# Batch 1's right-half product as seven half products, and a written-out order for all engines, in a gated cross-attention and FFN kernel

## The chip, the cores and the metric

The kernel runs on one core of one Trainium2 chip, in one launch. The metric is the device time of that launch in microseconds, the median of several runs. A profiled execution gives the trace; its span goes from the first to the last instruction of the program.

## What is computed

Two batches (`b` = 0, 1) of 1024 tokens with 2048 features go through two steps, both with a residual:

```python
x = x + tanh(g_xattn) * matmul(fake_quant(layernorm(x)), fake_quant(ctx))     # ctx: (2, 2048, 2048), one matrix for each batch
x = x + tanh(g_ffn) * scale * (x_ei @ kernel)                                  # x_ei: layernorm(x), its last 20% of features times -4
# fake_quant(v) = (clip(round(v / s + z), 0, 255) - z) * s
# kernel: (2048, 2048), of zeros and ones
```

"The first product" below is the one with the quantised context, "the second product" the one with the 0/1 matrix.

## The kernel before

The 16 tiles of 128 tokens are numbered `t` = 0 to 15 (8 to 15 are batch 1). Two neighbouring tiles form a pair `p`, two pairs a quad `q`. The result's columns are cut into four blocks `c` of 512; a half `h` is two blocks.

**First product, batch 0, and batch 1's right half (h = 1).** `load_x` brings a tile's rows, `stats` / `variance` / `square_root` / `factor` work out the layer norm (on VectorE, called DVE, and ScalarE, called ACT), `quant1` writes the quantised bytes, `turn1` transposes them on TensorE (PE), `take1` copies them from PSUM into an f16 tile `q1T`. `load_kv` and `quant_kv` do the same for the context; `fill_kv` on GpSimd (POOL) first clears the f16 tile that the bytes are written into. Column sums (`sums_mm` on PE, or `sums_pair` on DVE and `sums_last` on PE) and row sums (`rowsum1`, `rowsum1_pe`, then `tokb1`) correct for the zero points. `ops_unit` and `ops_several` give one unit of work: two tiles by one column block, 32 f16 matmuls of 128x512 (`mm1`), then for each tile `out1` (PSUM to SBUF, on ACT or DVE), `add_row1` and `add_out1` on POOL, `stats` for the second layer norm, and a store (`keep1`).

**First product, batch 1's left half (h = 0).** `ops_quad1` computes it with Strassen's scheme in Winograd's form: a pair of tiles and the two halves of the inner dimension make a 2x2 matrix of blocks, two column blocks and the same two halves another, and seven products of blocks (`mm1s`, M1 to M7) stand in for eight. `left_sum` and `right_sum` (DVE) make the sums and differences of blocks that these need. The seven products of a pair go into three PSUM sums X, Y, Z; after each product the running sum is added to where the scheme says: by `out1s` (ACT) and `add_out1` (POOL) for M2, M5, M4, M3, and by `take1s` (DVE) for M1, M6, M7.

**Second product.** `scale2`, `turn2` and `take2` normalise and transpose a tile (`A`); `combine` makes the left sums; `part_hi` (ACT) and `part_lo` (DVE or POOL) split each left block into two fp32r parts; `widen` (ACT) turns the bytes of the 0/1 matrix, or of its sums (`combine_w`), into fp32r; `mm2` runs seven products here too, in two passes (hi and lo). `add2` (DVE) adds a sum to rows loaded by `load_back`; `store2` writes them out.

**Memory.** SBUF holds 44 pages of 4 KB a partition, which all big tiles share. PSUM holds three accumulators of two banks each and two single banks for transposes and column sums.

**What sets the order.** The kernel first makes a list of steps: `op(...)` notes a step's engines with a cost on each, what it reads and writes, the pages it opens, and a due time. A planner in the kernel (`Plan.order`, `Plan.run`) then plays these steps through with those costs, 80 times with random changes of the due times, and keeps the order with the earliest end. Where a step may run on one of two engines, the planner chooses. The instructions are issued in that order, and each engine runs its own share strictly in turn; semaphores hold back what depends on another engine. All DMAs of the main part are issued from one queue, SyncE's (SP).

The lines that the prediction refers to by number:

```python
        nc.vector.tensor_sub(flat(out), flat(in0), flat(in1))                       # L609, right_sum
        nc.vector.scalar_tensor_tensor(xc, acc1[SUM[m], h, p // 2][:, p % 2, :], f1u, xc, ALU.mult, ALU.add)   # L658, take1s
```

L514 is `take1`, L544 `mm1`, L556 and L574 the column sums on PE, L646 `mm1s`, L692 `turn2`, L782 `widen`, L809 `mm2`, L825 `add2`.

Of the kernel before, what the change touches and what calls it, by code (L numbers as in the profile page):

```python
# [20 lines left out]
P = 128  # L21
# [8 lines left out]
class Op:  # L30
    __slots__ = ("engines", "f", "args", "deps", "users", "due", "lead", "opens", "uses",
                 "place", "end", "left", "index", "engine", "bias", "port", "ready")


class Plan:

    def __init__(self, buffers):
        self.free = dict(buffers)
        self.ops = []
        self.place = 0.0
        self.writer = {}  # L50
        self.readers = {}
        self.opener = {}
        self.kind = {}
        self.count = {}
        self.first = None

    def op(self, engines, f, *args, reads=(), writes=(), opens=(), main=False, due=None, lead=80, bias=0.0,
           port=False, in_turn=False):

        o = Op()
        o.engines, o.f, o.args, o.lead, o.index = engines, f, args, lead, len(self.ops)
        o.deps, o.users, o.uses, o.opens = set(), [], set(), []
        o.place, o.ready = None, 0.0
        o.due, o.bias, o.port = due, bias, port
        for kind, buf in opens:
            assert buf not in self.opener, buf
            self.opener[buf], self.kind[buf], self.count[buf] = o, kind, 0
            o.opens.append(buf)  # L70
        for key in reads:
            if key in self.writer:
                o.deps.add(self.writer[key])
            self.readers.setdefault(key, []).append(o)
            o.uses.add(key[0])
        for key in writes:
            if key in self.writer:
                o.deps.add(self.writer[key])
            o.deps.update(self.readers.pop(key, ()))
            self.writer[key] = o  # L80
            o.uses.add(key[0])
        for buf in o.uses:
            if buf in self.opener:
                o.deps.add(self.opener[buf])
                self.count[buf] += 1
        if in_turn:
            if self.first is not None:
                o.deps.add(self.first)
            self.first = o
        o.deps.discard(o)  # L90
        for d in o.deps:
            d.users.append(o)
        if main:
            o.place = self.place
            self.place += min(engines.values())
            o.due = o.place if due is None else due
        self.ops.append(o)
        return o

    def dues(self):  # L100
        inf = float("inf")
        given = [o.due for o in self.ops]
        for o in reversed(self.ops):
            d = inf if o.due is None else o.due
            for u in o.users:
                if u.place is not None or u.due is not None and u.due < inf:
                    d = min(d, (u.due if u.place is None else u.place) - min(o.engines.values()) - 3)
            o.due = d
        for o, g in zip(self.ops, given):
            if o.due == inf:  # L110
                o.due = max([d.due for d in o.deps] + [0.0]) + 50

    def order(self, lag, start, runs, seed=1):


        self.dues()
        chance = random.Random(seed)
        free, count = dict(self.free), dict(self.count)
        dues = [o.due for o in self.ops]
        best = None  # L120
        for i in range(runs):
            self.free, self.count = dict(free), dict(count)
            try:
                end = self.run(lag, start)
            except RuntimeError:
                end = None
            if end is not None and (best is None or end <= best[0]):
                best = end, self.began, [o.engine for _, _, o in self.began]
                dues = [o.due for o in self.ops]
                held = self.held_up()  # L130
            for o, due in zip(self.ops, dues):
                o.due = due
            for ops in held:
                if chance.random() < 0.5:
                    step = chance.choice((3.0, 6.0, 12.0, 24.0))
                    for o in ops:
                        o.due -= step
            if i % 3:
                place = chance.uniform(0.0, self.place)
                for o in self.ops:  # L140
                    if o.place is None and abs(o.due - place) < 120.0 and chance.random() < 0.1:
                        o.due += chance.uniform(-25.0, 25.0)
        _, self.began, engines = best
        for (_, _, o), e in zip(self.began, engines):
            o.engine = e
        return [o for _, _, o in self.began]

    def held_up(self):

        before, begin, all_ = {}, {}, []  # L150
        for s, _, o in self.began:
            begin[o] = s
            last = before.get(o.engine)
            before[o.engine], before[o] = o, last
            if o.place is None or last is None or s - begin[last] - last.engines["PE"] < 1.0:
                continue
            ops = []
            x = o
            for _ in range(8):
                x = self.rel.get(x)  # L160
                if x is None or x.place is not None:
                    break
                ops.append(x)
                p = before.get(x)
                if p is not None and begin[p] + p.engines[p.engine] > x.ready + 1.0:
                    break
            all_.append(ops)
        return all_

    def run(self, lag, start):  # L170


        self.rel = {}
        ready = {}
        events = []
        began = []
        for o in self.ops:
            o.left = len(o.deps)
            o.end = 0.0
        tick = 0  # L180

        def push(time, what, o):
            nonlocal tick
            tick += 1
            heappush(events, (time, tick, what, o))

        for o in self.ops:
            if not o.left:
                for e in o.engines:
                    push(0.0, "ready", (e, o))  # L190
        done = set()
        engines = sorted({e for o in self.ops for e in o.engines}, key=lambda e: (e != "PE", e))
        for e in engines:
            ready[e] = []
        busy = {e: e in start for e in engines}
        for e, time in start.items():
            push(time, "idle", e)
# [82 lines left out]
def gated_xattn_ffn_kernel(  # L280
# [885 lines left out]
    for q in (2, 3):  # L1166
        ops_quad1(0, q)
# [62 lines left out]
```

## Time and profile before

| | |
|---|---|
| median of 3 runs | 698.88 us (698.78 to 699.11) |
| span of the profiled execution | 697.0 us |
| PE busy | 674.0 us, 97% |
| PE weight loads | 471.7 us, beside the matmuls |
| DVE busy | 490.2 us, 70% |
| ACT busy | 455.4 us, 65% |
| POOL busy | 316.8 us, 45% |
| moved by DMA | 155.78 MB, 223 GB/s over the span |

The page gives the profiled execution by its span; the runs' median lies 1.9 us above that. The time of any one run lies within 0.3 us of the median. A span's stages by the start of their first instruction: the first matmul at 13.2 us; the second product of batch 0 from 145 us on; batch 1's first product from 367 us on (its right half mostly between 408 and 476 us); its second product from 476 us on. In groups of instructions, the time after the bar is what the group was busy, then the mean of one instruction in ns, then the idle time of the engine before it and what ended that. Instructions that follow each other on DVE and ACT overlap a little, so busy time over count is what one costs its engine, and the mean is what one lasts. In windows the columns are the length, then busy time (and count) of PE, its weight loads, DVE, ACT and POOL, the granted clock, the DMA share and GB/s.

### The profile page before, as it was taken

Reading aid. Unit: us, or ns where it says so; the run is one execution under the profiler, and the core shown is the slowest. Engines: PE = TensorE matmul, PEld = TensorE weight load, DVE = VectorE, ACT = ScalarE, POOL = GpSimd, SP = SyncE. Lnnn points to the kernel's source line nnn. Section 1 sums busy time; section 2 is a strip of 40 time slices with the busy share of each in tenths; the row PEclk is TensorE's granted clock in tenths of the full one; section 3 lists DMA queues with packets and bytes.
Section 4 is the critical chain, followed back from the end, with each engine's and each line's share of the span. In section 5 each row is a group of like instructions: output and inputs, shape, how many; then the busy total and the mean of one; then the engine's idle time right before and its main releaser. Section 6 shows DMA issues by size and latency. Waiting matters only on the chain.

```text
span 697.0 us, 8833 instructions
## 1 busy us (share of the span) xinstructions
PE 674.0 (97%) x3180; PEld 471.7 (68%) x3180; DVE 490.2 (70%) x717; ACT 455.4 (65%) x536; POOL 316.8 (45%) x210
## 2 busy tenths in 40 slices
PE   1999999989999999999999999999999999999997
PEld 0444444468788888878885444447888888888885
DVE  6899958899998886497878888468572425583331
ACT  4599444286888566699926768229699347689540
POOL 8166789863625221855717887975120101040000
PEclk9999999999999999999999999999999999999999
DMA  8999406777995799477379677327074379155032
GB/s 302 393 393 380 162 13 231 259 261 251 361 400 225 233 324 339 140 247 278 120 263 330 222 268 245 121 92 275 27 260 162 105 231 324 67 170 222 22 131 90
DMA packets 63580, 155.78 MB, mean 223 GB/s; under 512 B 4912, under 2 KB 21296, under 8 KB 63536
## 3 DMA queue, kind: packets, MB, share of 16 engines
q1 hardware_dynamic: 63536, 155.21, 62.9%
q8 instruction: 25, 0.41, 0.2%
q14 instruction: 19, 0.16, 0.1%
HBM read 117.44 MB, written 37.75 MB: 223 GB/s over the span
## 4 chain that ended last, share of the span: by engine, by line
PE 87%; DMA 4%; DVE 4%; POOL 2%; ACT 2%; issue 1%; SPq 0%; ACTq 0%; DVEq 0%
PE acc_M L809 57%; PE acc L544 19%; PE acc_M L646 7%; PE tr L692 4%; DMA kv<-in_kv_dram 3%; DMA x<-in_x_dram 1%; POOL x L596 1%; DVE wB L767 1%; ACT wf_M L782 1%; POOL x L592 1%; PE tr L503 1%; DVE qn L472 0%; PE cs L574 0%; DVE x L685 0%; DVE bn_b L426 0%
## 5 line engine op out<-in xcount | busy, mean ns | idle before, releaser
L809 PE MATMUL acc_M<-wf_M,hi_M 128*128 128x512 f32 x896 | 282.0, 395 | 1.6 <-ACT wf_M L782 1.5
L809 PE MATMUL acc_M<-wf_M,lo_M 128*128 128x512 f32 x896 | 277.6, 390 | 0.6 <-POOL lo_M L742 0.6
L782 ACT ACTIVATE wf_M<-wr_M 128x1024 fp32r<-128x1024 uint8 x224 | 221.6, 1050 | 26.8 <-DMA wr_M<-in_wmask_dram 24.2
L809 PEld LDWEIGHTS acc_M<-wf_M,lo_M 128*128 128x128 f32 x896 | 168.0, 188 | 36.8 <-POOL lo_M L742 1.3
L809 PEld LDWEIGHTS acc_M<-wf_M,hi_M 128*128 128x128 f32 x896 | 164.1, 188 | 34.4 <-ACT wf_M L782 3.2
L544 PE MATMUL acc<-q,q1T 128*128 128x512 f16 x768 | 171.6, 381 | 1.2 <-DVE q1T L514 0.8
L825 DVE SCALAR_TENSOR_TENSOR back<-acc_M,f,back 128x1024 f32<-128x1024 f32 (+1 forms) x58 | 72.1, 1245 | 124.7 <-PE acc_M L809 117.1
L742 POOL TENSOR_TENSOR lo_M<-A,hi_M 128x1024 fp32r<-128x1024 f32 x24 | 62.1, 2586 | 179.5 <-ACT hi_M L738 160.1
L544 PEld LDWEIGHTS <-q1T 128*128 128x128 f16 x768 | 75.2, 98 | 90.2 <-issue 1.9
L592 POOL TENSOR_TENSOR x<-x,row 128x512 f32<-128x512 f32 x64 | 88.6, 1408 | 43.8 <-ACT sd_a L438 15.5
L596 POOL TENSOR_TENSOR x<-x,e 128x512 f32<-128x512 f32 x64 | 92.0, 1458 | 30.6 <-ACT e L586 16.1
L738 ACT CAST hi_M<-A 128x1024 fp32r<-128x1024 f32 x48 | 50.1, 1044 | 13.1 <-POOL A L726 4.7
L530 ACT ACTIVATE q<-kv,sc,rs 128x1024 uint8<-128x1024 f32 x45 | 53.5, 1236 | 7.8 <-DMA kv<-in_kv_dram 5.1
L586 ACT ACTIVATE e<-acc,tokb,f1u 128x512 f32<-128x512 f32 x34 | 25.1, 774 | 49.6 <-PE acc L544 47.8
L426 DVE BATCH_NORM_STATS2 bn_b<-x 128x6 f32<-128x512 f32 x64 | 43.1, 684 | 15.9 <-POOL x L596 15.6
L495 ACT COPY A<-tr 128x512 f32<-128x512 f32 x35 | 20.3, 584 | 46.5 <-PE tr L692 45.8
L742 DVE TENSOR_TENSOR lo_M<-A,hi_M 128x1024 fp32r<-128x1024 f32 x24 | 33.7, 1421 | 7.2 <-ACT hi_M L738 7.2
L568 DVE TENSOR_TENSOR pair<-pair,q 128x1024 f16<-128x1024 f16 x36 | 36.6, 1022 | 2.5 <-ACT q L530 0.8
L728 POOL TENSOR_TENSOR A<-A,A 128x1024 f32<-128x1024 f32 x8 | 21.1, 2648 | 23.7 <-DVE A L726 16.4
L522 POOL MEMSET q<- 128x1024 f32 x32 | 29.2, 952 | 5.1 <-DVE q L532 2.2
L512 ACT ACTIVATE q1T<-tr 128x1024 f16<-128x1024 uint8 x22 | 21.3, 1019 | 7.5 <-PE tr L503 6.8
L767 DVE SCALAR_TENSOR_TENSOR wB<-wB,wB 128x2048 uint16<-128x2048 uint16 x8 | 24.2, 3031 | 0.0
(103 smaller groups left out, 594.1 us busy)
## 6 DMA issues: line engine op xcount, KB each, us to landing
kv<-in_kv_dram SPq DMA_DIRECT2D x64, 512.0 KB, 9.2
x<-in_x_dram SPq DMA_DIRECT2D x32, 512.0 KB, 7.7
x<-x SPq DMA_DIRECT2D x32, 512.0 KB, 3.0
back<-x SPq DMA_DIRECT2D x32, 512.0 KB, 6.1
wr_M<-wt_T SPq DMA_DIRECT2D x32, 512.0 KB, 5.6
out_dram<-back SPq DMA_DIRECT2D x30, 512.0 KB, 3.6
wr_M<-in_wmask_dram SPq DMA_DIRECT2D x24, 512.0 KB, 5.4
n<-in_x_dram SPq DMA_DIRECT2D x16, 512.0 KB, 7.2
```

The costliest lines, as they stand in the source:

```text
L426: nc.vector.bn_stats(bn[v, t][:, c, :], xt[src[v, t, c // 2]][:, ts(c % 2, NB)])
L530: nc.scalar.activation(low, v, AF.Identity, bias=z2, scale=rs2)
L544: nc.tensor.matmul(acc1[b, c, tiles[0]][:, i, :], q1T[tiles[i]][:, k, :], rhs1(b, c, k), start=(k == 0), stop=(k == KT - 1),)
L568: nc.vector.tensor_add(colsum[b, c], colsum[b, c], v[:, i : i + 2, :])
L592: nc.gpsimd.tensor_add(xc, xc, colrow[b, c])
L596: nc.gpsimd.tensor_add(xc, xc, ev.pop((t, c)))
L646: nc.tensor.matmul(acc1[key][:, i, :], left_half(p, LEFT1[m])[:, 4 * s + k, :], right1(m, h, s)[:, k, :], start=(m in OPENS and s == 0 and ...
L738: nc.scalar.copy(hi[m, p], A[left(m, p)])
L742: engines[engine].tensor_sub(lo[m, p], A[left(m, p)], hi[m, p].bitcast(F32))
L782: nc.scalar.activation(wf[q, m, k], wr[q, m, k // 4][:, k % 4, :], AF.Copy, bias=-float(RIGHT[m][1]))
L809: nc.tensor.matmul(acc2[SUM[m], p][j], part[m, p][:, k, :], wf[q, m, k][:, ts(j, NB)], start=(m in OPENS and k == 0 and part is hi), stop= ...
L825: nc.vector.scalar_tensor_tensor(v, acc, f2, v, ALU.mult, ALU.add)
```

## The change

Two things are changed together.

1. `ops_quad1` is called for both halves of batch 1, and `ops_right_sums(1, ...)` makes the right sums of the right half; the units (`ops_unit`) of that half and the early loads of its x tiles go. A tile's left sums, made once for the left half, are used again.
2. The planner is taken out of the kernel. `Plan` still notes the steps with their dependencies, but issues them in the order of a table, `ORDER_OF_OPS`, of 2326 step numbers; a letter behind a number says which engine takes a step that may run on two (D, A, P). Costs, due times and the limits on pages are no longer looked at.

The list of steps is otherwise the same: 2314 before, 2326 after (64 `mm1` and 16 `out1` go; 56 `mm1s`, 16 `out1s`, 12 `take1s` and 8 `right_sum` come). The order of the steps in the table is not that of the planner before.

```diff
-    def __init__(self, buffers):
-        self.free = dict(buffers)
+    def __init__(self):
...
-    def dues(self):
...
-    def order(self, lag, start, runs, seed=1):
...
-    def held_up(self):
...
-    def run(self, lag, start):
...
+    def run(self, order):
+
+        names = {"D": "DVE", "A": "ACT", "P": "POOL"}
         done = set()
...
+        for word in order.split():
+            o = self.ops[int(word.rstrip("DAP"))]
+            assert o not in done and o.deps <= done
+            done.add(o)
+            if len(o.engines) > 1:
+                o.f(*o.args, engine=names[word[-1]])
             else:
...
+                o.f(*o.args)
+        assert len(done) == len(self.ops)
+
+
+ORDER_OF_OPS = """
+0 1 33 16 17 90 32 40 149 35 37 38 48 195 42 3 43 2 45 207 4 5 143 47 18 85 6 19 7 87 95 8 213 59 34A 155 20 9A
+84 229 41D 137 21 10A 58 22 23 36A 11 24 89 12A 231 50 44D 25A 220 13D 221 92 39A 26D 14 52 49A 46D 222 223 15
...
-    plan = Plan(dict(page=PAGES, acc=3, tr=2, qn=QN, row=4, e=3, pair=2))
+    plan = Plan()
...
     for c in range(2, NC):
         ops_kv(1, c, 200.0, False)
+    ops_right_sums(1, 200.0)
     pairs = ops_batch(1, "x", True)
-    for q in (2, 3):
-        ops_quad1(0, q)
-    for t in range(TPB, T):
-        v = ("x", t, 1)
-        op({"SP": DMA}, load_x, v, t, 1, writes=both(v), opens=[("page", v)], lead=60)
-    for some in (pairs[:2], pairs[2:]):
-        for c in range(2, NC):
-            for tiles in some:
-                ops_unit(1, c, tiles)
+    for h in range(2):
+        for q in (2, 3):
+            ops_quad1(h, q)
     ops_left(2, (False, False))
     ops_product2(2, {4: [(ops_left, (3, (True, True)))]})
     ops_product2(3, {})
 
-    order = plan.order({("ACT", "SP"): 8.0, ("POOL", "SP"): 12.0, ("DVE", "SP"): 12.0, "PE": 6.0, "ACT": 1.5, "DVE": 1.5, "POOL": 1.5, "SP": 4.0, "DMA": 10.0,
-                        ("PE", "PE"): 0.0}, {"SP": 13.0, "DVE": 22.0, "ACT": 22.0}, 80, 2)
-    for o in order:
-        if len(o.engines) > 1:
-            o.f(*o.args, engine=o.engine)
-        else:
-            o.f(*o.args)
+    plan.run(ORDER_OF_OPS)
```

## The prediction

> **What bounds it now.** I read the page's shares first, then the chain that ended last in order of time, then the windows, then the forms of VectorE (DVE), and last the built order of both kernels.
>
> ```profile
> PE 674.0 (97%) x3180; PEld 471.7 (68%) x3180; DVE 490.2 (70%) x717; ACT 455.4 (65%) x536; POOL 316.8 (45%) x210
> ```
>
> TensorE (PE) is busy for 97%. Its steady paces are in the chain and the timeline:
>
> ```profile
> 42.74 1.13 DVE q1T L514
> ...
> 77.99 18.99 PE acc L544 x88
> ...
> 506.40 70.77 PE acc_M L809 x312
> ```
> ```profile
> 13.23 1.01 PE L556 MATMUL cs<-q,ones_h 128*128 128x512 f16 x2 [13.23 <-ACT q L530]
> ...
> 19.06 2.61 PE L544 MATMUL acc<-q,q1T 128*128 128x512 f16 x6
> ...
> 692.60 0.75 DVE L825 SCALAR_TENSOR_TENSOR back<-acc_M,f,back 128x512 f32<-128x512 f32 x1 [1.06 <-PE acc_M L809]
> ```
>
> One f16 matmul takes 18.99 / 88 = 0.2158 us, one of the second product 70.77 / 312 = 0.2268; eight transposes take 0.87 in the chain, 0.109 each; 16 row sums 0.54, 0.034 each. PE's whole list at these paces: 1792 x 0.2268 + (768 + 224 + 44) x 0.2158 + 320 x 0.109 + 32 x 0.034 = 406.4 + 223.6 + 34.9 + 1.1 = 666.0. The last eviction starts at 692.6, so PE ends 26.6 us "late" against its list. I follow that lateness by counting the matmuls ahead of a place: 13.2 before the first matmul; 20.0 at 44.6 us (the first matmuls take 2.61 / 6 = 0.43, and PE waits for the DVE step in the chain at 42.74); still 20.1 at 138.3 (tile 0's first transposes); 23.7 at 254.6 (tile 6's first transposes); 26.6 at the end. After the first 45 us PE loses 6.6 us in all. Nothing else can give much: the end is 697.0 - 692.6 = 4.4 of eviction and store.
>
> Second thing to see: how well DVE can be filled.
>
> ```profile
> 25.00:75.00 50.00, 48.45 (x258) 22.96 (x257) 48.07 (x95) 42.91 (x46) 29.09 (x22) 1.00 1.02 381
> 75.00:125.00 50.00, 50.00 (x237) 23.21 (x236) 37.81 (x94) 20.03 (x31) 41.47 (x34) 1.00 0.36 125
> 150.00:200.00 50.00, 48.47 (x236) 39.42 (x235) 48.71 (x67) 40.48 (x51) 22.81 (x10) 1.00 0.94 329
> ```
>
> Third column of time is DVE. Pressed (first and third row) it is busy 96.78 of 100 us, idle 3.3% of its busy time; unpressed (second) it idles 32%. In the first 25 us it is busy 18.38, of which 1.8 are constants: it starts 8.4 us behind its list.
>
> **What goes and comes on PE.** The right half took 4 pairs x 2 columns x 32 = 256 matmuls (64 steps of 4); as seven products it takes 4 x 7 x 8 = 224 (56 steps). 32 x 0.2158 = 6.9 us leave PE, and PE sets the end. The rest of its list is the same. This is the whole gain of the arithmetic; 1.0% of 698.88.
>
> **What the seven products add.** The left half shows all of it.
>
> ```profile
> L658 DVE SCALAR_TENSOR_TENSOR x<-acc_M,f1u,x 128x512 f32<-128x512 f32 x12 | 8.5, 744 | 4.5 <-PE acc_M L646 2.2 <-issue 2.2
> ...
> L609 DVE TENSOR_TENSOR q2T<-q,q 128x2048 f16<-128x2048 f16 x2 | 6.8, 3430 | 0.0
> ...
> L609 DVE TENSOR_TENSOR q<-q,q 128x2048 f16<-128x2048 f16 x2 | 2.4, 1218 | 0.0
> ```
>
> DVE gets 12 take1s (8.5) and 8 right sums, at 1.22 each alone or 3.43 beside a 2.6 us GpSimd (POOL) subtraction: 9.8 to 27.4. I take 1.75, the mean of the eight here: 14.0. The 16 out1 of the right half (12 on ACT, 4 on DVE) become 16 out1s on ACT (11.7 us); POOL's adds stay 32. Pages: six more for the sums, 44 in all as before. Place: between the second column sum of batch 1 (C: PE list 324.5) and its second product (445.4) PE has 120.9 us, and in the new order DVE has 105 to do there with the right sums at 1.75. With the eight at 3.43 it is 119: still under PE, so I cost the additions at nothing; PE is the cover. Without the cover (DVE already behind at C) they would cost up to their 22.5. PSUM: 28 evictions instead of 16, each product of a sum waiting for the one before; the left half's two quads raise PE's lateness by 0.5 us (25.1 to 25.6), so 0 to 0.5 here, taken as 0.
>
> The Trainium skill, "SBUF — State Buffer", section "Who interferes with whom", speaks against these sums: a DVE instruction with two SBUF inputs and a GpSimd instruction that reads SBUF exclude each other for a whole instruction. The stage is POOL's busiest, but its adds there last 1.4 us, so by the rule a sum costs up to an estimated 2.7, less than the 3.43 seen.
>
> **The order table.** No instruction keeps its place after the first few: the order is new on all engines, from the first microseconds. DVE goes from 490 to 527 steps, ACT from 513 to 495: beyond the 20 steps above, DVE takes over quantising of kv (19 to 26), of x (11 to 16), take1 (10 to 16) and take2 (16 to 25), and gives up 7 out1 (those four among them) and 2 row sums. With busy/count of the forms (stats 0.65, quant kv 1.05, quant x 1.33, take1 1.19, row sum 2.26, out1 0.81, pair sums 0.87 and 2.03, scale2 1.19, lo part 1.37, combine 1.54, weight sum 3.03, add2 1.28, factor 1.70 and 0.80, variance 0.41, tokb 0.24, take2 0.68) the old list sums to 510.9 where the engine was busy 490.2, as neighbours overlap: factor 0.96. The new list is 548.9 x 0.96 = 527: below PE's 659.1. Whole sums do not decide; what is due when does. So I add up what DVE must have done before a given PE step: in DVE's new queue, everything up to the last instruction that the step waits for, directly or through other engines:
>
> - A, tile 0's transposes, now after 400 f16 matmuls instead of 524: PE list 91.3. DVE: 50 stats 32.5, 10 variances 4.1, factors 14.4, 10 kv 10.5, 8 take1 9.5, 6 quant 8.0, 3 row sums 6.8, 6 out1 4.9, pair sums 13.9, 2 scale2 2.4, 6 tokb 1.4: 108.4 x 0.96 = 104.1.
> - B, tile 6's transposes: PE list 228.6. DVE: 93 stats 60.5, variances and factors 37.5, 10 kv 10.5, 12 quant 16.0, 9 take1 10.7, 5 row sums 11.3, pairs 13.9, 10 tokb 2.4, 7 out1 5.7, 15 scale2 17.9, 8 weight sums 24.2, 7 lo 9.6, 5 combines 7.7, 5 take2 3.4, 12 add2 15.4: 246.6 x 0.96 = 236.7 (before: 214.0 at list 230.9).
>
> DVE reaches a place at 8.4 + list x (1 + idle share). At 3.3%: A at 116.0, PE lateness at least 116.0 - 91.3 = 24.7; B at 253.0, lateness 24.4; C (322.7) at 341.8, 17.3. So the new order makes DVE, not PE, the pace of the first 115 us: 4.6 us more lateness at A than the 20.1 there now. What PE lost between A and B (3.6) I take as hidden by that, since ACT and POOL gain the same 4.6. What it lost after B is 2.9; the transposes that caused part of it are spread differently now, so between 0 and 2.9: I take the middle, 1.5. End: 24.7 + 1.5 = 26.2 against 26.6.
>
> Loads: the 47th DMA (kv of column 2) is needed at PE list 49.5, that is at 69.5 with lateness 20. The windows move 331, 393 and 369 GB/s per 25 us, so 47 x 0.524 MB are in at about 68, and quantised 1.24 later: just in time. One load later costs 0.5 / 0.37 = 1.4 us. A new wait on SP would hold all loads behind it; the DMA count is unchanged.
>
> **Sum**, against the profiled execution (span 697.0; the runs' median lies 1.9 above): 697.0 - 6.9 - 0.4 + 1.9 = 691.6. Own range: idle share 2.6% (third row), nothing lost after B: lateness 23.9, -2.7, so 689.3; idle share 4.0% (first row) and 2.9 lost: B 26.0, lateness 28.9, +2.3, so 694.3.
>
> **Rivals.**
> 1. DVE becomes the bound (slower). The price: at B each 1% of idle share is 2.4 us on PE. 6.9 + 26.6 - 1.5 = 32.0 of lateness at B eats the gain; that is an idle share of 6.5%. For it: 105 us of the old order idle at 32% or near, because in-order DVE waits for POOL and ACT, and two operand forms grow from 1.2 to 3.4 beside POOL. Against it: 3.3% in pressed windows. At 8%: B at 264.0, lateness 36.9, +3.4: 702.3. Between 4% and 6.5% the time is 694 to 699.
> 2. DVE is less pressed than my averages (its conversions fall where POOL idles: 0.8 instead of 1.2). Then PE's lateness stays near 20.1 and gets at most the 2.9: 685.5 to 689.
> 3. The change does not do what it says: the 28 evictions hold PE. At 0.5 us for each of 14 products it gives the 6.9 back: about 699. The left half says 0.5 for the same number.
>
> The Trainium skill, "TensorE: Matmul & The Clock Gate", part 1, adds a risk to rival 1: after about 3.4 us of idleness PE runs at half rate for as long again. By it a relapse would cost an estimated 3.4 us. Here only the start shows the half pace; waits of up to 1.4 us later (ACT wf_M) brought none back.
>
> **Numbers.** Forecast 0.62; rival 2 0.14; milder DVE waits (694 to 699) 0.11; rival 1 0.10; rival 3 0.03. About 0.2% can be told from no change (697.5 to 700.3). Faster 0.83, same 0.05, slower 0.12. Range 687.5 to 699.0.
>
> **Checks.** In the profile after: 512 f16 matmuls of the plain form and 448 of the sevens; DVE busy about 527 and over 95% up to 115 us; tile 0's transposes at about 116, tile 6's at about 253; PE from C to the second product without gaps. I am wrong if PE waits for DVE several us near B, or if kv loads end its waits at 45 to 75 us.

## The result, and the profile after

The changed kernel takes 715.57 us, the median of four runs (711.99 to 717.09), against 698.86 us before: 1.0232 times as long, with a 95% interval of 1.0206 to 1.0257. The forecast was 691.6, with a range of 687.5 to 699.0. The profiled execution took 711.99 us with a span of 709.9: it is the fastest of the four, so that 3.6 of the median's 16.7 us stand in no trace. One execution of the first kernel below took 1166 us and one of the kernel with norms later 1782, and as these were the traced ones, the times of these two kernels are medians of the other three and no lateness is given for them.

The page's busy times, after:

```profile
PE 670.9 (95%) x3148; PEld 467.1 (66%) x3148; DVE 506.3 (71%) x753; ACT 445.0 (63%) x521; POOL 324.5 (46%) x211
```

32 matmuls fewer on PE, as foreseen, and no other engine that is near full. The chain that ended last, as shares of the span by engine, before and then after:

```profile
PE 87%; DMA 4%; DVE 4%; POOL 2%; ACT 2%; issue 1%; SPq 0%; ACTq 0%; DVEq 0%
```
```profile
PE 60%; DVE 16%; DMA 15%; issue 3%; ACT 2%; POOL 2%; SPq 1%; DVEq 0%
```

Before, PE carried the chain almost alone. After, DVE and loads carry a third of it, with little more work to do. The chain in order of time shows how (start, length, what):

```profile
94.06 6.04 PE acc L447 x28
...
264.40 5.08 DMA n<-in_x_dram
269.69 8.46 DMA y<-x
278.18 0.81 DVE y L588
...
409.44 5.20 DMA kv<-in_kv_dram
414.71 1.10 issue
415.81 1.44 ACT e L568 x2
417.32 1.58 POOL x L499
418.90 0.90 POOL q L425
419.82 1.25 ACT q L433
422.00 8.49 DMA kv<-in_kv_dram
...
664.52 41.11 PE acc_M L712 x180
```

The paces are those of before: 6.04 / 28 = 0.2157 and 41.11 / 180 = 0.2284 us a matmul. Between them stand relays: a load, a step of DVE, the next load (264 to 279 us), or a load of kv, an eviction, an add of GpSimd (POOL), a zero fill, a quantization, another load (409 to 430 us). No relay holds PE for long, since there is always some other product to run, but each costs a little: PE's waits in the whole execution, apart from the 13.2 us of the start, are some thirty that the trace names, none over 2.0 us.

The three stretches that the prediction read for DVE's idle share, and the two ends of PE's work:

```profile
25.00:75.00 50.00, 45.95 (x231) 21.28 (x229) 46.10 (x86) 38.23 (x42) 29.24 (x21) 1.00 1.03 391
75.00:125.00 50.00, 48.54 (x233) 22.98 (x233) 48.31 (x93) 20.35 (x29) 39.99 (x30) 1.00 0.41 139
150.00:200.00 50.00, 47.76 (x226) 38.26 (x224) 40.85 (x70) 34.40 (x43) 25.98 (x13) 1.00 0.71 244
```
```profile
13.18 1.01 PE L459 MATMUL cs<-q,ones_h 128*128 128x512 f16 x2 [13.18 <-ACT q L433]
...
705.65 0.75 DVE L728 SCALAR_TENSOR_TENSOR back<-acc_M,f,back 128x512 f32<-128x512 f32 x1 [1.06 <-PE acc_M L712]
```

DVE's idle share is 8.5%, 3.5% and 22% of its busy time. The rows of the added work (after, both halves together):

```profile
L561 DVE SCALAR_TENSOR_TENSOR x<-acc_M,f1u,x 128x512 f32<-128x512 f32 x24 | 17.5, 741 | 3.1 <-POOL x L495 2.4 <-PE acc_M L549 0.6
L512 DVE TENSOR_TENSOR q2T<-q,q2T 128x2048 f16<-128x2048 f16 x8 | 11.6, 1455 | 1.6 <-PE acc_M L712 1.4 <-PE acc_M L549 0.2
L512 DVE TENSOR_TENSOR q2T<-q,q 128x2048 f16<-128x2048 f16 x4 | 6.8, 1695 | 0.0
L512 DVE TENSOR_TENSOR q<-q,q 128x2048 f16<-128x2048 f16 x4 | 6.5, 1656 | 0.0
```

The sums are cheap: (11.6 + 6.8 + 6.5) / 16 = 1.56 us each where 1.75 had been taken.

The prediction's own measure reads best: PE's lateness, that is the start of a PE step less the sum of PE's list ahead of it. The table below gives it at places of the list, worked out from the traces in the same way as there and good to some 0.2 us (units: the right half as it was; sevens: as in the change). The right half's products stand at 382 to 445 of the list (to 450 with units), with the left half's last ones among them, up to 396.

| kernel | 100 | 150 | 250 | 345 | 375 | 405 | 435 | 460 | 655 | time |
|---|---|---|---|---|---|---|---|---|---|---|
| before (units) | 20.1 | 22.9 | 24.2 | 25.1 | 25.6 | 25.6 | 25.6 | 25.6 | 26.3 | 698.9 |
| after (sevens) | 25.3 | 28.3 | 35.2 | 36.7 | 37.1 | 39.7 | 41.9 | 43.0 | 46.2 | 715.6 |

6.9 us of matmuls are saved and 46.2 - 26.3 = 19.9 us of lateness are added (13.0 together, which is what the profiled execution is longer), spread over the whole program: the two differ by 5.2 at 100, 11.0 at 250, still 11.5 at 375, then 16.3 at 435 and 19.9 at the end.

### The profile page after: what moved, and what is told of

Read it like the earlier page. It is cut to its first block, busy times and chain, and to the rows that moved or that the text cites. A ratio compares the mean times of both kernels' runs of the same rounds, so it can differ in the third digit from the quotient of the medians.

```text
span 709.9 us, 8788 instructions
## 1 busy us (share of the span) xinstructions
PE 670.9 (95%) x3148; PEld 467.1 (66%) x3148; DVE 506.3 (71%) x753; ACT 445.0 (63%) x521; POOL 324.5 (46%) x211
## 4 chain that ended last, share of the span: by engine, by line
PE 60%; DVE 16%; DMA 15%; issue 3%; ACT 2%; POOL 2%; SPq 1%; DVEq 0%
PE acc_M L712 44%; PE acc L447 7%; DMA kv<-in_kv_dram 7%; PE acc_M L549 6%; DMA y<-x 4%; PE tr L595 3%; DVE pair L471 3%; DMA x<-in_x_dram 3%; DMA n<-in_x_dram 2%; DVE bn_b L329 2%; ACT wf_M L685 1%; DVE back L728 1%; DVE q2T L512 1%; POOL x L499 1%; DVE bn_a L329 1%
## 5 line engine op out<-in xcount | busy, mean ns | idle before, releaser
L645 POOL TENSOR_TENSOR lo_M<-A,hi_M 128x1024 fp32r<-128x1024 f32 x23 | 56.4, 2454 | 208.6 <-ACT hi_M L641 142.5
L495 POOL TENSOR_TENSOR x<-x,row 128x512 f32<-128x512 f32 x64 | 94.7, 1495 | 53.9 <-ACT row L481 34.8
L447 PE MATMUL acc<-q,q1T 128*128 128x512 f16 x512 | 116.7, 381 | 1.8 <-ACT q L433 1.4
L499 POOL TENSOR_TENSOR x<-x,e 128x512 f32<-128x512 f32 x64 | 96.9, 1526 | 31.8 <-ACT e L489 13.7
L447 PEld LDWEIGHTS <-q1T 128*128 128x128 f16 x512 | 49.9, 98 | 61.0 <-issue 1.9
L433 ACT ACTIVATE q<-kv,sc,rs 128x1024 uint8<-128x1024 f32 x38 | 46.7, 1238 | 35.4 <-DMA kv<-in_kv_dram 33.1
L549 PEld LDWEIGHTS <-q1S 128*128 128x128 f16 x256 | 24.9, 98 | 30.8 <-DVE q1S L533 1.4
L329 DVE BATCH_NORM_STATS2 bn_b<-x 128x6 f32<-128x512 f32 x64 | 42.3, 680 | 0.0
L489 ACT ACTIVATE e<-acc,tokb,f1u 128x512 f32<-128x512 f32 x25 | 19.3, 772 | 25.3 <-PE acc L447 22.7
L549 PEld LDWEIGHTS <-q1T 128*128 128x128 f16 x192 | 18.7, 98 | 23.7 <-issue 2.4
L568 ACT ACTIVATE e<-acc_M,tokb,f1u 128x512 f32<-128x512 f32 x32 | 23.5, 769 | 15.0 <-POOL x L499 8.9
L435 DVE TENSOR_SCALAR q<-kv,rs,sc 128x1024 uint8<-128x1024 f32 x26 | 26.0, 1010 | 7.9 <-DMA kv<-in_kv_dram 7.1
```

What stands on the lines that cost most here:

```text
L329: nc.vector.bn_stats(bn[v, t][:, c, :], xt[src[v, t, c // 2]][:, ts(c % 2, NB)])
L433: nc.scalar.activation(low, v, AF.Identity, bias=z2, scale=rs2)
L447: nc.tensor.matmul(acc1[b, c, tiles[0]][:, i, :], q1T[tiles[i]][:, k, :], rhs1(b, c, k), start=(k == 0), stop=(k == KT - 1),)
L495: nc.gpsimd.tensor_add(xc, xc, colrow[b, c])
L499: nc.gpsimd.tensor_add(xc, xc, ev.pop((t, c)))
L549: nc.tensor.matmul(acc1[key][:, i, :], left_half(p, LEFT1[m])[:, 4 * s + k, :], right1(m, h, s)[:, k, :], start=(m in OPENS and s == 0 and ...
```

## Experiments

Two things were changed together, so the theories were: **1**, the sevens are a gain and the table's order is what costs; **2**, the sevens of the right half cost more beside PE than they save, whatever the order; **3**, the table gives DVE too much work. All of before's times in these runs lie at 698.7 to 698.9. Where an experiment changes the order alone, the table of steps is what changes, and a few words of it stand for the diff.

### Is it the table?

**Sevens, but ordered by the planner of before:**

```diff
     for c in range(2, NC):
         ops_kv(1, c, 200.0, False)
+    ops_right_sums(1, 200.0)
...
-    for q in (2, 3):
-        ops_quad1(0, q)
...
+    for h in range(2):
+        for q in (2, 3):
+            ops_quad1(h, q)
```

> Both halves as seven products, the order made by the planner of before (80 tries, its costs unchanged). Theory 1, the written-out order is what costs and the seven products are a gain: 698.9 less 6.9 of matmuls plus 0 to 3 of new waits, 692 to 695, and PE's lateness against its list stays near 27 us. Theory 2, the seven products of the right half cost more than they save (28 evictions, 8 right sums on VectorE): 703 or more, with PE's waits gathered in batch 1's first product.

712.97 us (1.0201, 1.0183 to 1.0220). Theory 1 missed by some 20 us: without the table the sevens are as slow.

**The table's order and engines with units in the right half** (64 unit steps where the 56 products stood, steps that they need pulled forward):

```diff
-    ops_right_sums(1, 200.0)
...
-    for h in range(2):
-        for q in (2, 3):
-            ops_quad1(h, q)
+    for q in (2, 3):
+        ops_quad1(0, q)
...
+    for some in (pairs[:2], pairs[2:]):
+        for c in range(2, NC):
+            for tiles in some:
+                ops_unit(1, c, tiles)
```

> The order of the table and its choice of engines, but batch 1's right half as units of before: their 64 matmul steps stand at the places of the 56 steps of the sevens, each out1 and its two additions right behind the unit (22 steps were pulled forward for that). Theory 1: the order's waits stay, 6.9 us of matmuls come back, less the about 4 us of waits that the sevens' stage had in the table: 713 to 721. Theory 2: 698 to 702.

722.41 us (1.0344, 1.0327 to 1.0362). Against after, 722.4 - 715.6 = 6.8: on the same order the sevens save about the 6.9 of the matmuls, though the runs of the two kernels spread over 2.6 and 5.1 us. But this order was made for sevens, so it says nothing on what an order for sevens costs.

**70 steps back from DVE to ACT**, places unchanged:

```diff
-84 229 41D 137 21 10A 58 22 23 36A 11 24 89 12A 231 50 44D 25A 220 13D 221 92 39A 26D 14 52 49A 46D 222 223 15
+84 229 41A 137 21 10A 58 22 23 36A 11 24 89 12A 231 50 44D 25A 220 13A 221 92 39A 26D 14 52 49A 46A 222 223 15
```

> The table's order unchanged, but the 70 steps that it moved from ScalarE to VectorE (19 quantising of kv, 19 take2, 13 take1, 10 quantising of x, 6 out1, 3 row sums) go back to ScalarE. Theory 3, VectorE has too much to do: about 60 us of work leave it and PE's waits for it go, 697 to 705. Theory 1, the places in the queues and not the amount are what costs: 709 to 722, as ScalarE now holds these steps at places that were not chosen for it.

734.79 us (1.0512, 1.0497 to 1.0528), PE's lateness 54.5 at 310 of the list; PE now waits mostly for ACT. This is above what either theory said: an order is bound to its engines, and the run doesn't settle theory 3 by itself. That falls with the order of before below, which leaves DVE as much to do (505.7 us busy, 506.3 in the table's) and is no faster.

**The table up to the first matmul of batch 0's second product, the planner's order behind it:**

```diff
-579 620 523 611D 580A 524 435 458D 690 525 608 562 592 1151 437 634 512A 1188 754 593A 594 621 635 459 595D 563
...
+579 620 523 611D 580A 524 435 458D 690 525 608 562 592 1151 437 436 441 442 443 459 460 465 466 464 467 461 482
...
```

> Sevens in both halves; the table's order up to the first matmul of batch 0's second product, then all other steps in the planner's order of the first kernel of this call. Theory 1: the table's first stage has PE about 4.4 us later than before at that place (25.3 against 20.9), the rest is as in the planner's: 695 to 700. Theory 2: as the planner's kernel, 703 or more.

712.69 us (1.0201, 1.0186 to 1.0216). Not 695 to 700: the planner's second part is worth 2.9 us, less than the 5.1 over which the table's runs spread.

**Another draw of the planner**, for units and for sevens: the last number in the call below.

```diff
-                        ("PE", "PE"): 0.0}, {"SP": 13.0, "DVE": 22.0, "ACT": 22.0}, 80, 2)
+                        ("PE", "PE"): 0.0}, {"SP": 13.0, "DVE": 22.0, "ACT": 22.0}, 80, 1)
```

Units:

> The kernel before with nothing changed but the seed of its planner (1 in place of 2): the same work in another order. Theory 1 as it stands after the first four runs (an order for this work is worth 5 to 20 us, and before has a lucky one): 704 to 720 us. Rival (the planner finds an equally good order for the units whatever its seed, and only the new list of work is hard to order): 697 to 701 us.

Sevens:

> Sevens in both halves, ordered by the kernel before's planner with seed 1 in place of the 2 of the first run of this study (713.6 us). Theory 1: another draw from a spread of orders, 697 to 720 us, and more than 2 us from 713.6. Rival (the work itself costs the 20 us): 711 to 716 us again.

Units 698.94 us (1.0002, 0.9992 to 1.0011), sevens 713.16 us (1.0208, 1.0189 to 1.0228). Only 237 of DVE's 490 steps stand at the same place in the two unit orders, and the time is the same: before's order was no lucky one, and 713 is no unlucky one. Theory 1 falls. Planned alike, units against sevens is 14 us; the table adds some 2 to that, within the spread of its runs.

| kernel | 100 | 150 | 250 | 345 | 375 | 405 | 435 | 460 | 655 | time |
|---|---|---|---|---|---|---|---|---|---|---|
| units, other draw | 20.1 | 22.9 | 23.7 | 24.0 | 25.3 | 25.3 | 25.3 | 25.4 | 26.1 | 698.9 |
| sevens, other draw | 21.6 | 25.5 | 28.2 | 29.5 | 37.7 | 40.9 | 45.1 | 45.8 | 46.3 | 713.2 |

Against units, the planner's sevens lose 15 of their 20 us from 345 to 460, around the right half; 7.8 of these are one wait, at 413 us, of a left-half product for a left sum of DVE. The table loses 11 of its 20 earlier. The sum is the same.

### The order of before with sevens

**The whole order of before kept**, the 56 products in the places of the 64 unit steps:

```diff
-0 1 33 16 17 90 32 40 149 35 37 38 48 195 42 3 43 2 45 207 4 5 143 47 18 85 6 19 7 87 95 8 213 59 34A 155 20 9A
...
+33 38 43 0 48 1 85 16 90 2 95 17 3 100 4 32 5 137 6 35 18 143 7 19 37 8 149 34A 155 40 20 9A 195 21 42 22 201
...
```

> The sevens of the right half, but in the order and on the engines that the kernel before has: 1412 of its 1422 shared steps of VectorE, ScalarE, GpSimd and the loads stand at the same place against TensorE's list as before, the 56 products stand where the 64 matmul steps of the units stood, and only the steps of the right half itself (its eight sums, twelve writing evictions, sixteen evictions and what follows them) stand as in the changed kernel's table. Theory 1 (the arithmetic is a gain and the table's order is what costs): 692 us (before less the 6.9 us of matmuls), 690 to 696. Theory 2 (the products of halves cost more beside TensorE than they save, whatever the order): 703 us or more.

717.63 us (1.0272, 1.0257 to 1.0287): theory 2. And the loss now has a place. This order on the table's engines:

```diff
-36D 10A 229 45 207 23 39A 24 47 11 41A 213 231 50 233 25D 12A 235 84 26D 13A 44D 46A 52 220 49D 221 222 51D 53
+36A 10A 229 45 207 23 39A 24 47 11 41D 213 231 50 233 25A 12A 235 84 26D 13D 44D 46D 52 220 49A 221 222 51D 53
```

> The same order as the run before it in this call, but each step that may go to more than one engine goes to the engine that the table gives it: 149 shared steps change engine. If what the table costs is who does what, this comes out near the changed kernel (710 to 718 us); if it is where a step stands in its queue, near the run before it in this call (692 to 698 us). An assignment that was not made for this order can cost by itself, so a time in between settles neither.

740.05 us (1.0591, 1.0574 to 1.0609): worse than either, as with the 70 steps above, so it doesn't tell place from engine. **Three parts**, before's order, the table from batch 1's first left-half product to its second product, before's order again:

```diff
-1137 1341 1333 1138 1139 1354 1337 1140 1357 1143 1141 1144 1414 1145 1420 1146 1147 1417 1426 1415 1148 1423
...
+1335 1136 1137 1341 1333 1138 1418 1139 1354 1337 1369 1140 1357 1143 1141 1392 1398 1367 1144 1414 1415 1145
...
```

> A version that might beat both, all of the work done: the order of the kernel before up to the first product of batch 1's left half, the changed kernel's table from there to batch 1's second product, and the order of the kernel before again for what is left. Adding up how late TensorE ran in each part where that order was used (25 us in the first, 5.2 in the second, 0.7 in the third, and 6.3 from its last matmul to the end of the run) on a list of 659 us: 696.4 us. Theory 2a: 694 to 702, since each order keeps to its own part. Rival (an order is worth only what stood before it, and the parts don't fit): 706 us or more.

714.53 us (1.0228, 1.0213 to 1.0244): the rival. In the table below 8 us go at the first seam (33.7 at 345), and 8.3 more between 375 and 405: the table's cheap right half rests on what it had done before.

| kernel | 100 | 150 | 250 | 345 | 375 | 405 | 435 | 460 | 655 | time |
|---|---|---|---|---|---|---|---|---|---|---|
| before's order, sevens | 20.2 | 23.0 | 24.4 | 25.2 | 25.7 | 33.3 | 42.9 | 51.7 | 52.4 | 717.6 |
| three parts | 19.9 | 22.8 | 24.1 | 33.7 | 38.3 | 46.6 | 47.3 | 47.3 | 48.7 | 714.5 |

With before's order PE is as late as before up to 375 of the list, and loses 26 us from there to 460. PE's waits of that kernel between 405 and 500 us (total, times, longest):

```profile
PE acc_M L712 <- ACT wf_M L685: 5.8, 1, 5.8
PE acc_M L549 <- ACT e L568: 3.9, 2, 2.8
PE acc_M L549 <- DVE x L561: 3.5, 2, 1.9
PE acc_M L549 <- ACT q L433: 2.8, 2, 1.5
```

Evictions (`e`, `x`), quantizations (`q`) and, at the second product's start, widened weights (`wf_M`). The engines behind them are not full. Stretches of 25 us, before and then this kernel (PE, weight loads, DVE, ACT, POOL, clock, DMA share, GB/s):

```profile
435.00:460.00 25.00, 25.00 (x117) 11.33 (x116) 13.15 (x36) 4.94 (x10) 22.99 (x19) 1.00 0.41 149
460.00:485.00 25.00, 25.00 (x128) 15.76 (x126) 18.96 (x39) 17.80 (x27) 14.63 (x11) 1.00 0.48 162
```
```profile
435.00:460.00 25.00, 19.60 (x83) 8.19 (x82) 18.63 (x21) 6.98 (x8) 16.30 (x12) 0.93 0.29 107
460.00:485.00 25.00, 23.06 (x112) 10.98 (x111) 17.52 (x30) 8.59 (x15) 20.53 (x16) 1.00 0.32 105
```

GpSimd is the fullest of them at the end: its adds into x take 58.8 us between 400 and 500 us before and 59.8 here, but the last one ends at 479.5 us before (3 us into the second product) and at 494.0 here (7 us into it). In the table's order it ends at 495.3 (8 us into it), in the planner's at 492.1 (3 us, as before). The units took column 2 first, and column 3 was quantized at 394 to 406 of the list while they ran. The sums of the sevens need both columns, so products and evictions come later, and GpSimd's adds with them: that is the reading which the next runs test.

### What holds PE in that order

Three kernels take one thing each out of it (in the first two, steps that had waited for it stand earlier). **No supply** (the products of the right half run on zeros):

```diff
     def load_kv(b: int, c: int, g: int):
+        if b == 1 and c >= 2:
+            return
...
     def quant_kv(b: int, c: int, g: int, engine=None):
+        if b == 1 and c >= 2:
+            return
```

> The run in the order of the kernel before (717.6 us: exactly as late as before until TensorE's list stands at 375 us, and 26 us later by 460) with the supply of its right half left out: the 16 loads and 16 quantizations of kv columns 2 and 3 of batch 1 are not done, and the zero fills of their pages stand 20 to 40 us earlier, since nothing holds them up; the eight sums, 56 products, 28 evictions and all of GpSimd's adds stay. The products run on zeros there. Theory 2a (products of halves need both columns of kv before the first of them, where the units needed column 2 first and column 3 only halfway, so loads and quantizations press into the left half's time): 692 to 699 us. Theory 2b (the right half's own evictions, 28 in place of 16, with GpSimd's adds behind them, hold TensorE's three banks): 708 us or more.

**Quantizations but one load:**

```diff
     def load_kv(b: int, c: int, g: int):
+        if b == 1 and c >= 2 and (c, g) != (2, 0):
+            return
...
-        v = flat(stage[b, c, g])
+        v = flat(stage[1, 2, 0] if b == 1 and c >= 2 else stage[b, c, g])
```

> The same as the run before it in this call, but the 16 quantizations are done, at the earlier places and on the engines of the kernel before; they all read the one load that is kept, so that 15 loads with their pages of on-chip memory are still left out. If loads and pages are what holds the supply up: within 3 us of the run before it. If it is the engines' time for the quantizations (some 20 us of ScalarE and VectorE within 35): 5 us or more above it.

**No adds by GpSimd:**

```diff
     def add_row1(b: int, c: int, t: int):
+        if b == 1 and c >= 2:
+            return
...
     def add_out1(c: int, t: int):
+        if c >= 2 and t >= TPB:
+            ev.pop((t, c))
+            return
```

> The run in the order of the kernel before (717.6 us) with the 32 adds of GpSimd in the right half left out (the row of column sums and the evicted products are not added to x there), everything else, the supply too, as it was. Theory 2b: 695 to 705 us. Theory 2a: 711 us or more, since the products still wait for the columns.

| kernel | 345 | 375 | 405 | 435 | 460 | 655 | time | ratio |
|---|---|---|---|---|---|---|---|---|
| before's order, sevens | 25.2 | 25.7 | 33.3 | 42.9 | 51.7 | 52.4 | 717.6 | 1.0272 |
| no supply | 25.2 | 29.4 | 31.8 | 37.3 | 45.2 | 45.8 | 711.7 | 1.0186 (1.0171 to 1.0201) |
| quantizations, one load | 25.1 | 35.2 | 35.2 | 40.7 | 48.6 | 49.3 | 715.6 | 1.0242 (1.0225 to 1.0259) |
| no adds by GpSimd | 25.1 | 25.6 | 34.6 | 35.4 | 42.3 | 43.0 | 708.2 | 1.0132 (1.0117 to 1.0147) |

Each theory explains a part: neither 2a nor 2b holds as stated. Without the supply 5.9 us go; the 16 quantizations bring 3.9 of them back, so the loads are worth 2. Without GpSimd's adds 9.4 us go, nearly all between 405 and 435 (0.8 lost there in place of 9.6), and the 9 us up to 405 and the 7 after 435 stay. All four lose 7 to 9 us from 435 to 460, where the second product starts. For these, SyncE's queue in the kernel with before's order gave a suspect (start, length, DMA issues):

```profile
485.96 8.41 SPq L575 DMA_DIRECT2D x<-x  x5
494.46 0.38 SPq L723 DMA_DIRECT2D back<-x  x1
494.90 1.45 SPq L681 DMA_DIRECT2D wr_M<-in_wmask_dram  x2
```

Five stores of x wait for GpSimd, and weights stand behind them that went out at 472 and 479 us before.

### Can order alone take it away?

Each kernel but the planner's adds one remedy to the one ahead of it, and all of the work is done. **Weights ahead of the stores:**

```diff
-1618 1666 1667 1655 1664 1668 1603 1669 1665 1656 1673 1620 1676 1621 1677 1624 1622 1678 1670 1626 1679 1650
+1782 1666 1667 1655 1664 1668 1603 1669 1665 1656 1673 1783 1620 1676 1621 1677 1624 1622 1678 1670 1679 1650
```

> The order of the kernel before with sevens (717.6 us), with the weight loads of the second product's first three matrices 14 us of TensorE's list earlier in SyncE's queue, the stores of the right half's x later, behind them, and the first widening of weights 6 us earlier. All of the work is done. If the 7 us at the start of batch 1's second product are weights queued behind stores: 709 to 712 us. If something else holds TensorE there: 715 us or more.

**Rows after the evictions:**

```diff
-                for j in range(2):
-                    op({"POOL": GPS(NB)}, add_row1, 1, 2 * h + j, t, reads=[(("row", 1, 2 * h + j), 0)], writes=[(v, j)],
+                for j in range(2):
+                    if h in EARLY_ROWS:          # EARLY_ROWS = (0,)
...
+                    if h not in EARLY_ROWS:      # behind a block's last eviction
+                        op({"POOL": GPS(NB)}, add_row1, 1, 2 * h + j, t, reads=[(("row", 1, 2 * h + j), 0)],
```

> As the run before it in this call, and in the right half GpSimd's 16 adds of the row of column sums come after a block's evictions in place of before them, so that no eviction that adds into x waits for the row. If the row adds in front of the evictions are what costs: 5 to 9 us below the run before it. If GpSimd's time for its 32 adds is what costs, whichever comes first: within 2 us of it.

**Left half first, quantizations earlier** (table lines only):

```diff
-1346 1458 1497 1244A 1459 1492 1466 1347 1467 1493 1273 1468 1460 1503 1472 1462 1469 1506 1274A 1461 1463 1507
+1495 1346 1458 1244A 1459 1492 1466 1347 1467 1493 1273 1468 1460 1503 1472 1462 1469 1506 1355 1274A 1461 1463
```

> As the run before it, and the left half's last products come before the first of the right half, with the quantizations of kv columns 2 and 3 some 12 us earlier (370 to 392 us of TensorE's list in place of 382 to 405) where pages allow it. If the three costs are separate and order alone takes them away: 692 to 699 us. If the earlier quantizations only press on the left half, as in the runs with a thinned supply: 702 us or more.

**The planner with rows after the evictions** (`EARLY_ROWS = ()` in the planner's kernel with sevens):

```diff
+    EARLY_ROWS = ()
```

> Sevens in both halves by the planner with seed 1 (713.2 us), with the row of column sums added after a block's evictions in both halves. If GpSimd's row adds in front of the evictions cost in the planner's order too (its chain of waits had 22% of 385 to 480 us in GpSimd's adds): 703 to 709 us. If not: 711 us or more.

**Norms later** (table lines only):

```diff
-1800 1775D 1745 1789 1717 1699 1700 1635 1637 1638 1639 1726 1701 1703 1718 1669 1727 1728 1729 1693 1641 1642
+1775D 1745 1789 1717 1699 1700 1635 1726 1718 1727 1728 1641 1642 1643 1719 1720 1790 1746A 1747 1802 1637 1638
```

> The run with all three remedies (716.9 us), with the variances, square roots and factors of the tiles 9, 11 and 12 to 15 behind the copies of transposes that TensorE needs first, 4 to 14 us of TensorE's list later in VectorE's and ScalarE's queues. If the place of those norms in the queues is what holds TensorE: 703 to 708 us. If the loss moves on to the next thing that GpSimd's late adds hold up: 712 us or more.

**Eight rows on VectorE:**

```diff
-        nc.gpsimd.tensor_add(xc, xc, colrow[b, c])
+        (nc.vector if c >= 2 and t >= 12 else nc.gpsimd).tensor_add(xc, xc, colrow[b, c])
```

> As the run before it in this call, with GpSimd's adds of the row of column sums for tiles 12 to 15 in the right half (8 of its 32 adds there, 1.26 us each, 10 us in all) done by VectorE. If GpSimd's time is what is left: 3 to 8 us below the run before it. If VectorE's added 6 to 10 us cost as much: within 2 us of it or above.

| kernel | 345 | 375 | 405 | 435 | 460 | 655 | time | ratio |
|---|---|---|---|---|---|---|---|---|
| weights first | 25.2 | 25.7 | 33.3 | 40.9 | 50.1 | 50.9 | 715.9 | 1.0244 (1.0229 to 1.0259) |
| + rows after | 24.9 | 25.4 | 34.2 | 36.3 | 53.5 | 54.2 | 721.0 | 1.0327 (1.0298 to 1.0355) |
| + left first, quantizations earlier | 24.9 | 27.7 | 33.3 | 33.3 | 50.2 | 50.8 | 716.9 | 1.0261 (1.0243 to 1.0278) |
| + norms later | | | | | | | 714.6 | 1.0227 (1.0210 to 1.0244) |
| + eight rows on VectorE | 25.1 | 27.9 | 33.7 | 33.7 | 42.0 | 44.9 | 710.6 | 1.0169 (1.0152 to 1.0185) |
| planner, rows after | 33.5 | 33.5 | 41.6 | 44.6 | 45.7 | 46.3 | 713.4 | 1.0205 (1.0190 to 1.0220) |

The four remedies of order (weights, rows, left first, norms) miss what was hoped for and say the same: the loss that one clears at its own place turns up at the next. Weights were not what held the second product's start: with them ahead, 9.2 us still go from 435 to 460. With all three, PE stands at 33.3 from 405 to 435, where the order of before had lost 9.6 us, and then loses 17 at once. PE's wait in that kernel, and ACT's queue ahead of the copy that it waits for:

```profile
493.53 1.12 PE L595 MATMUL tr<-ident,x 128*128 128x128 f32 x4 [10.06 <-ACT A L398]
```
```profile
484.08 0.78 ACT L568 ACTIVATE e<-acc_M,tokb,f1u 128x512 f32<-128x512 f32 x1 [1.83 <-POOL x L499]
491.76 0.20 ACT L341 ACTIVATE sd_b<-va_b 128x1 f32<-128x1 f32 x1 [6.90 <-DVE va_b L336]
491.87 1.04 ACT L685 ACTIVATE wf_M<-wr_M 128x1024 fp32r<-128x1024 uint8 x1
492.82 0.19 ACT L341 ACTIVATE sd_b<-va_b 128x1 f32<-128x1 f32 x1
492.91 0.56 ACT L398 COPY A<-tr 128x512 f32<-128x512 f32 x1
```

A square root for a later tile's norm waits 6.9 us for DVE, DVE for GpSimd's adds, which run without a gap from 480 to 493.1 us; the copy for PE stands behind it. Moving these norms back gives 2.2 us, not 9 to 14. Taking 8 of the 32 adds off GpSimd gives 4.0 us more, within the 3 to 8 expected; its last add then ends at 486.9. Whether the row is added before or after the evictions is no matter in the planner's order (713.4 against 713.2) and costs 5 us in the other; less work for GpSimd is what helps. None of these kernels beats before. The best with all of the work done is 710.6.

## Why the prediction was wrong

**Right.** The 6.9 us of the list: 3148 matmul records for 3180, and 6.8 us on the same order. Checkpoint A: tile 0's transposes at 116.8 us, lateness 25.3, for 116.0 and 24.7. The loads are as tight as said: a kv load stands in the chain up to 53 us, and lateness goes from 20.3 at 45 us to 25.3 at 93.5. DVE is not full, 506.3 us for 527. That A came out is in part luck:

```profile
0.00:116.80 116.80, 95.57 (x469) 44.41 (x470) 104.60 (x212) 69.88 (x80) 76.84 (x71) 1.00 0.76 276
```

DVE was idle for 2.1 us more than allowed (8.5% and then 3.5% where 3.3% had been taken), and what it did up to there, 104.6 less 1.8 of constants, was 1.3 us less than the 104.1 summed.

**The step that failed most: the additions "at nothing", with PE as the cover.** The left half, whose two quads cost 0.5 us, was taken as the pattern. But the left half finds its columns of kv quantized, and the units of the right half were the light stage at whose start columns 2 and 3 were quantized and in which GpSimd's adds and the norms for the second product were done. The sum counted DVE's 105 us of work in 120.9 us of PE, took GpSimd's adds as unchanged because they stay 32, and left out what is due when. With before's order kept, that stage costs 26 us more (25.7 at 375, 51.7 at 460); without GpSimd's adds in it 9.4 of them go, without the loads and quantizations of columns 2 and 3 5.9. Every order tried with all of the work done pays 18.6 us or more in all: the planner's 15 of its 20 around the stage itself, the table's 20 spread.

**"What PE lost between A and B I take as hidden".** From A to B lateness grew from 25.3 to 32.3 (tile 6's transposes at 261.0 us, not 253.0), and from B to the end to 46.2 where 1.5 had been taken. A checkpoint that adds up DVE's work sees DVE's whole sum, not the relays between DVE, the loads and PE of the chain at 264 to 279 us. Even with before's own losses in these stretches, 3.6 and 2.9, the end would have been 25.3 + 6.5 = 31.8.

**The rivals.** Rival 1 priced 702.3 for a DVE that binds at B. Its threshold, 32.0 of lateness at B, was met (32.3), its mechanism was not: the stretch from 150 to 200 us leaves DVE idle for 22%, and taking 70 steps off DVE made it 19 us slower. Rival 3, the 28 evictions holding PE, had the right place and a chance of 0.03; at 0.5 us for each product it was priced at about a quarter of the 26 us. It lacked GpSimd behind the evictions. Rival 2, a DVE less pressed, fell at A already (25.3, not 20.1).

**The clock.** The prediction weighed "TensorE: Matmul & The Clock Gate", part 1 of the Trainium skill. In the changed kernel no wait after the start is over 2.0 us and the granted clock stays at 1.00 in all of the stretches shown. In the kernel with before's order and sevens, matmuls go at half pace after a wait of 2.79 us, and the next twelve after one of 5.78 us (start, length, [wait]; then a window inside the first):

```profile
442.45 4.39 PE L549 MATMUL acc_M<-q,q1S 128*128 128x512 f16 x12 [2.79 <-ACT e L568]
...
494.48 1.22 PE L712 MATMUL acc_M<-wf_M,hi_M 128*128 128x512 f32 x2 [5.78 <-ACT wf_M L685]
495.50 1.05 PE L712 MATMUL acc_M<-wf_M,lo_M 128*128 128x512 f32 x2
496.36 1.05 PE L712 MATMUL acc_M<-wf_M,hi_M 128*128 128x512 f32 x2
```
```profile
443.00:445.00 2.00, 2.00 (x7) 0.62 (x6) 1.63 (x3) 0.53 (x1) 0.00 (x0) 0.50 0.00 0
```

At the second, two take 0.86 us from start to start, and the twelve 5.29 (494.48 to 499.77) instead of 12 x 0.2268 = 2.72: 2.6 us. The first costs 1.6, and a third, after waits of 1.48 and 1.31 us at 410 us, 1.5. So nearly 6 of the 26 us that this kernel loses in the stage are half pace, not waits; the clock of 0.93 in the stretches above belongs to the first. Of the 9.4 us that go without GpSimd's adds, 7.8 are waits and 1.5 half pace. The page's rule (half rate after some 3.4 us of idleness) agrees with the wait of 5.78 us, but not with that of 2.79; with eight rows on VectorE the half clock came beside waits of 2.16 and 2.38 us, and with left first it didn't after one of 2.98 at 414.5 us. The price of 3.4 us for a relapse was too high: 3.4 us at half pace lose 1.7, and the relapses here cost 1.5 to 2.6.

**What stays open.** Shown is that a kernel with sevens in the right half was slower than before in every order tried, where the time is lost when nothing else is moved, and what leaving out GpSimd's adds or the supply gives back. Leaving out both was not tried, and the waits and half pace that stay without GpSimd's adds (9 us up to 405 of the list, 7 after 435) are not explained by a run. That another order, or another share of GpSimd's work, would make them pay is not excluded; the last step, eight adds moved, still gave 4 us. Why the table's order is 11.6 us behind before at 345 of the list was only read from its chain, not tested by itself: it issues kv loads of batch 1 up to 170 us ahead of where the planner has them, and DVE and loads carry its chain there.

## What to carry to other kernels

A stage in which the bounding engine does plain, slow work is where the other engines do the next stage's work. Before it is made shorter, list for every engine and queue, the slowest adder included, what is done beneath it and from when it can be done: work saved there is only a gain if its lodgers find another place. Where engines take their queues in order, a remedy for one wait shows the next: a cost is understood when leaving the work out gives the time back, not when one wait has gone.

## What was not expected of the hardware

GpSimd's adds of 128x512 f32 take 1.26 to 1.27 us each when they run one behind the other (32 in the right half, 40 us at that pace), 70% more than VectorE's evicting adds of the same size (0.74). The changed kernel's four runs spread over 5.1 us and those of the planner's other draw of sevens over 3.5, ten runs of the other unit order over 0.12. Why was not tested; the sevens in before's order spread over 0.9 only. The half clock came beside waits of PE of 2.2 to 3.0 us in some places and not in others.
